# A graph-network layer: message groups in pairs, and a second layer with the features on partitions

## The chip, the cores and the metric

The kernel runs on one core of a Trainium2 chip, in one launch. The metric is the time of one execution on the device, in microseconds, as the median of several runs. A profiled execution gives the span (from the first to the last recorded instruction) and the trace from which the durations below come.

## The reference, cut to what matters

12,500 nodes with 64 features, 200,000 edges sorted by their target node. Each edge makes a message from its own features and from the features of its two nodes; messages are summed at the target node; a small network and a layer norm finish the nodes.

```python
x      (12500, 64)      edge_attr_64 (200000, 64)      edge_weight1 (200000, 1)
src, dst (200000,)      # dst is sorted
ssp(v) = softplus(v) - log(2)

nodes       = x[stack(src, dst)].reshape(E, 128)
gates       = ssp(edge_attr_64 @ We1 + be1) @ We2 + be2          # (E, 64)
gates       = gates * (1 - sigmoid(5 * (edge_weight1 - 3.5)))    # the cut
h           = ssp(nodes @ Wn1 + bn1) @ Wn2 + bn2                 # (E, 64)
message_sum = zeros(12500, 64).at[dst].add(h * gates)
new_state   = x + (ssp(message_sum @ Ws1 + bs1) @ Ws2 + bs2)
out         = layernorm(x + new_state)
```

## The kernel before

**Tiling.** Edges are worked off in 391 groups of 512 (`NG`). A group is two halves of 256 edges (`HE`); in each half the targets fall in a window of 42 consecutive nodes (`W`). Edges of a group also stand as four tiles of 128 (`K`), edge on the partition. All values are float32.

**A group's way.** Source rows come in by `gather`: four indirect DMAs on POOL (L231), one for each tile of 128 edges, into a buffer `xg` of which there are `AHEAD + BEHIND` = 19. Some 47 of the 1564 tiles are brought row by row by small DMAs on the queues of SP and ACT (`fetch`, L257). VectorE writes a one-hot of the target in its window beside the rows (`onehot`, L293). PE transposes the four tiles of 106 columns (`transposes`, L307), and ACT copies the result from PSUM to SBUF (`xcopy`, L314, the tile `xT`). Layer 1 is then feature-major, features on partitions and edges along the free side: a bias matmul of three bf16 pieces (`layer1_bias`, L319), the edge part (`layer1_edge`, L324) and two node matmuls (`layer1_node`, L330) whose weights `wns` hold Wn1's source half and, below it, 42 rows of a table `x @ Wn1` (target half) for the window; the one-hot rows pick from it. The table is made in the prologue (L591) and its rows are loaded by SP (L286).

Softplus is exp (`exps`, L341) and log with a bias of one (`logs`, L344) on ACT over 768 columns, and one min/max operation on VectorE (`softplus`, L349).

Layer 2 of before is edge-major: the softplus tile is the stationary operand and the small weights move, 2 matmuls for the edge net (L361) and 4 for the node net (L366), onto a bias matmul of 512 columns (L354). VectorE multiplies by the cut (`hcut`, L375) and makes the message (`message`, L379). PE sums the messages into the windows with the one-hots as moving operand (`scatter`, L383), and VectorE adds each half's 42 columns to the running sums (`window`, L400), whose address is read from a table of window bases.

**The order of the work.** Engines' queues are in the order in which the code is written. The loop `for i in range(-1, last - 1)` issues layer 1 of group i+1, layer 2 of group i and the scatter of group i-2, so that a group's parts are spread over three turns. In the last `CLOSE` = 12 turns the scatter is one group behind instead. `load(i + LOADS)` puts edge features and window tables on SP's queue five groups ahead, behind a scatter long past. `gather(i + AHEAD)` stands fourteen groups ahead on POOL; a buffer of rows is free again when the scatter of the group 19 before has read its one-hots. Row DMAs on ACT's queue stand between its activations (`fetch(i, 1, 3)`), on SP's seven to a group. As node sums become complete, 25 node blocks of the last network and the layer norm (`node_block`, split in parts that `BLOCK_STEPS` spreads) are put between the groups. The last groups are finished after the loop by code of their own.

PSUM: `z_tile` (layer 1, two banks), `gh_tile` (layer 2) and `tx_tile` (transposes) come from rotating pools. The scatter's result uses free columns of a `z_tile`.

Of the kernel before, what the change touches and what calls it, by code (L numbers as in the profile page):

```python
# [42 lines left out]
F32 = mybir.dt.float32  # L43
# [4 lines left out]
OP = mybir.AluOpType  # L48
# [19 lines left out]
LOADS = 5  # L68
SPREADS = 5
PREPARE = 5  # L70
BEHIND = 5
CLOSE = 12


BLOCK_STEPS = ((2, 3, 4, 4, 6, 7, 8, 9, 10, 14), (2, 3, 3, 4, 5, 6, 7, 8, 9, 10), (1, 2, 1, 2, 3))
# [48 lines left out]
def gnn_resnorm_kernel(ctx: ExitStack, tc: tile.TileContext, a: dict, out: bass.AP, E: int):  # L124
# [53 lines left out]
    one = const.tile([P, 1], F32, name="one")  # L178
    half = const.tile([P, 1], F32, name="half")
    eps = const.tile([P, 1], F32, name="eps")  # L180
    ones3 = const.tile([PIECES, HE], BF16, name="ones3")
    be3 = const.tile([PIECES, 2, D], BF16, name="be3")
    row3 = const.tile([PIECES, 2, K, D], BF16, name="row3")
    rs3 = const.tile([PIECES, K, D], BF16, name="rs3")
    wns = const.tile([DW, REST, 2, 2 * D], F32, name="wns")

    xgs, xrs, eTs = {}, {}, {}
    made = {}

    def note(key, ins):  # L190
# [80 lines left out]
    bases = {}  # L271

    def load(g):
        old = ("scatter", g - LOADS - 4)
        if g % 2 == 0:
            n = min(2, NG - g)
            both = loads.tile([P, 2, HE], F32, name="eT", bufs=4)
            behind(note(("load", g), nc.sync.dma_start(both[:, :n], a["eT"][:, g : g + n, :])), old)
            for j in range(n):
                eTs[g + j] = both[:, j]  # L280
            _, at = nc.values_load_multi_w_load_instructions(
                base_i[32:33, 2 * g : 2 * g + 4], engines=[SP], min_val=0, max_val=8 * D * (N - 1),
                skip_runtime_bounds_check_because="they were clamped to these bounds")
            bases[g], bases[g + 1] = at[:2], at[2:]
        for h in range(2):
            behind(note(("load", g), nc.sync.dma_start(  # L286
                wns[D:DW, g % REST, h, :].bitcast(U8),
                table_bytes[:, bass.ds(bases[g][h], 8 * D * W)].rearrange("o (w f) -> (o w) f", w=W))), old)
# [27 lines left out]

    def layer1_bias(g, *needs):
        zs[g] = z_tile()
        first = nc.tensor.matmul(zs[g][:, 0, :HE], be3.rearrange("q h d -> q (h d)"), ones3, start=True, stop=False,  # L319
                                 skip_group_check=True)  # L320
        behind(first, *needs)

# [14 lines left out]

    def exps(g, part=every):
        if part.start == 0:
            us[g] = work.tile([P, 3 * HE], F32, name="u")  # L340
        nc.scalar.activation(us[g][:, part], z_of(g)[:, part], AF.Exp)  # L341

    def logs(g, part=every):
# [1 line left out]

    def softplus(g, part=every):
        if part.start == 0:
            ss[g] = work.tile([P, 3, 2, P], F32, name="s", bufs=3)
        nc.vector.scalar_tensor_tensor(ss[g].rearrange("p i t e -> p (i t e)")[:, part], us[g][:, part], BIG,  # L349
                                       z_of(g)[:, part], OP.min, OP.max)  # L350

# [23 lines left out]
        nc.vector.tensor_mul(hs[g], ghs[g][:, 1], cut[:, g, :].to_broadcast([P, K, D]))  # L375

    def message(g):
        msgs[g] = work.tile([P, K, D], F32, name="msg", bufs=3)
        nc.vector.tensor_mul(msgs[g], ghs[g][:, 0], hs[g])  # L379

    def scatter(g, sc):
# [13 lines left out]
    def window(g):  # L395
        if g not in window_at:
            window_bases(g)
        for h in range(2):
            part = sums[h * D : (h + 1) * D, bass.ds(window_at[g][h], W)]
            nc.vector.tensor_add(part, part, scs[g][h * D : (h + 1) * D, h * W : (h + 1) * W])  # L400

    def node_block(first, n, pool):

# [86 lines left out]
    with tc.manual_schedule():  # L490
# [4 lines left out]
        with tc.tile_pool(name="prep", bufs=1) as prep:  # L495
# [81 lines left out]
                    nc.vector.tensor_sub(rest, rest, pieces[:, q, :])  # L577
            nc.scalar.dma_start(row_d.rearrange("(o q) f -> o q f", o=1), pieces)
            rows = prep.tile([PIECES, 4, D], BF16, name="rows")
            nc.scalar.dma_start(rows.rearrange("q i d -> q (i d)"), row_d)  # L580
            for i in range(3, PARTS):
                load_x(i)
# [3 lines left out]
            for i in range(PARTS):  # L586
                for c in range(i * CP, (i + 1) * CP, CP // 2):
                    m = CP // 2
                    ps = z_tile().rearrange("p b (k f) -> p (b k) f", k=K)
                    for k in range(m):  # L590
                        nc.tensor.matmul(ps[:, k, :], xT[:, c + k, :], wnb, start=True, stop=True)  # L591
                    tb = prep.tile([P, m, 2 * D], F32, name="tb", bufs=6)
                    nc.scalar.copy(tb[:, :K, :], ps[:, :K, :])
                    nc.vector.tensor_copy(tb[:, K:, :], ps[:, K:m, :])
                    nc.sync.dma_start(by_node[:, c : c + m], tb)
                    nc.vector.memset(sums[:, c * P : WIDE if c + m == NCH else (c + m) * P], 0.0)
                if i == 1:
                    nc.vector.tensor_copy(base_i[:1], base_b[:1])
                    nc.vector.tensor_scalar(base_i[32:33], base_b[32:33], float(8 * D), None, OP.mult)
                    nc.vector.tensor_scalar(rows_i, rows_i, float(4 * D), None, OP.mult)  # L600
                    for k in range(2):
                        nc.vector.tensor_copy(be3[:, k, :], rows[:, 0, :])
                    for k in range(K):
                        nc.vector.tensor_copy(row3[:, :, k, :], rows[:, 1:3, :])
                        nc.vector.tensor_copy(rs3[:, k, :], rows[:, 3, :])
                if i == 2:
                    nc.scalar.activation(dist, dist, AF.Sigmoid, bias=steep, scale=-5.0)
                    nc.scalar.preload_act_table_set("natural_log_exp_and_others")
                    nc.vector.tensor_copy(rel, dst_i)
                    for t in range(2):  # L610
                        r = rel[:, :, 2 * t : 2 * t + 2]
                        nc.vector.tensor_sub(r, r, base_b[:, :NH].rearrange("p (g h) -> p g h", h=2))


        with tc.tile_pool(name="finish", bufs=1) as finish:
            blocks = list(zip(node_blocks(N), block_steps(N, NG)))
            last = NG - 1
            parts, begun, complete, rest = {}, None, 0, []

            def at(f, g, *more):  # L620
                if 0 <= g < NG:
                    f(g, *more)

            def behind_by(i):
                close = last - CLOSE
                return [g for g in ([i - 2] if i <= close else []) + ([i - 1] if i >= close else []) if g >= 0]

            for g in range(LOADS - 1):
                load(g)
            for g in range(2):  # L630
                onehot(g)
            for i in range(-1, last - 1):
                now = parts.pop(i, [])
                early = [part for part in now if part.tensor]
                at(load, i + LOADS)
                read_rows(i, 0, ROWS[0])
                fetch(i, 0, ROWS[0])
                if i >= 0:
                    at(gather, i + AHEAD)
                transposes(i + 1, ("load", i + 1), ("gather", i + 1), ("onehot", i + 1))  # L640
                xcopy(i + 1)
                read_rows(i, 1, ROWS[1])
                fetch(i, 1, ROWS[1] - 6)
                layer1_bias(i + 1)
                at(layer2_bias, i)
                for n, g in enumerate(behind_by(i)):
                    scatter(g, zs[i + 1][:, 1, HE + 2 * n * W : HE + 2 * (n + 1) * W])
                layer1_edge(i + 1)
                layer1_node(i + 1)
                exps(i + 1)  # L650
                fetch(i, 1, 3)
                logs(i + 1)
                fetch(i, 1, 3)
                for g in behind_by(i):
                    window(g)
                at(layer2, i)
                for part in early:
                    part.tensor(tx_tile())
                at(hcut, i)
                at(message, i)  # L660
                softplus(i + 1)
                for part in early:
                    part.others()
                at(onehot, i + 3)
                for part in now:
                    if not part.tensor:
                        part.others()
                complete = i
                if blocks and complete >= blocks[0][1] - PREPARE and not begun:
                    begun = node_block(*blocks[0][0], finish)  # L670
                    begun.pop(0).others()
                if blocks and complete >= blocks[0][1]:
                    steps = next(steps for steps in BLOCK_STEPS if i + steps[-1] < last - 1)
                    for n, part in zip(steps, begun):
                        parts.setdefault(i + n, []).append(part)
                    rest = begun[len(steps) :]
                    blocks.pop(0)
                    begun = None
            assert len(blocks) == 1 and begun and not parts


# [43 lines left out]
    with tc.If(far > 0), tc.tile_pool(name="outside", bufs=1) as o:  # L725
# [7 lines left out]
        with tc.For_i(0, NG, 1) as g:  # L733
# [20 lines left out]
            for k in range(K):  # L754
# [1 line left out]
            xT = o.tile([P, NB], F32, name="xT2")  # L756
            nc.vector.tensor_copy(xT, z[:, 0, :])
            z = z_tile()
            nc.tensor.matmul(z[:, 1, :HE], be3.rearrange("q h d -> q (h d)"), ones3, start=True, stop=False,
                             skip_group_check=True)  # L760
            nc.tensor.matmul(z[:, 1, :HE], we1.rearrange("a h d -> a (h d)"), e, start=False, stop=True,
                             skip_group_check=True)
# [110 lines left out]
```

## Time and profile before

| What | Value |
|---|---|
| time, median of 3 runs | 2687.81 us (2668.61 to 2691.71) |
| the profiled execution's own time | 2686.47 us |
| its span | 2684.7 us |
| mean granted TensorE clock | 0.815 of full speed |
| PE busy | 2243.6 us (84%), 11373 matmuls |
| ACT busy | 969.6 us (36%) |
| DVE (VectorE) busy | 1052.4 us (39%) |
| POOL busy | 1441.8 us (54%), 1520 instructions |
| first copy of xT, last copy of xT | 143.3 us, 2660.5 us |
| last gather ends | 2586.9 us |

A profile line of a group reads: line, engine, operation, what it writes and reads, shape, count; then busy time and mean ns of one; then the idle time of the engine just before such instructions, and what ended most of it. "PEld" are the weight loads of PE, "ACTq" and "SPq" the queues' issues. "remote" is a release that the profile can't put down to an instruction. The granted clock tells how much of TensorE's full speed the chip allowed; a busy share means less at half clock.

### The profile page before, as it was taken

To read this page: it belongs to the slowest core of one execution; us is meant where nothing else is said; L and a number is where in the kernel's file an instruction comes from. 1 tells how busy PE (TensorE), PEld (TensorE's weight loads), DVE (VectorE), ACT (ScalarE), POOL (GpSimd) and SP (SyncE) were. 2 spreads that over 40 slices of the span, in tenths; PEclk is the share of its full clock that TensorE was granted. 3 is DMA by queue.
4 is the path that set the end of the run, shared out by engine and by line. 5 is a ranking of instruction groups with operands and counts; after the bars stand their busy time and mean duration, and the time that the engine had idled before them with its cause. 6 is when DMAs were issued, how large, how long until landed. Compare 5 with 4: busy or idle time off the path is not lost.

```text
span 2684.7 us, 47845 instructions
## 1 busy us (share of the span) xinstructions
PE 2243.6 (84%) x11373; PEld 1754.9 (65%) x11373; DVE 1052.4 (39%) x2767; ACT 969.6 (36%) x1318; POOL 1441.8 (54%) x1520
## 2 busy tenths in 40 slices
PE   2489888988888888888889788888888888888897
PEld 1467666766666666666667666666666667666676
DVE  1233333333334333344333443434433443444445
ACT  0133333333333333333333333333334333333344
POOL 7335555555555555555555555555555555555520
PEclk9987788788788778788777888778878887787878
DMA  6222222222222212222222222222222222222210
GB/s 159 82 64 52 48 51 49 48 49 48 49 52 50 49 47 51 51 52 47 52 46 50 51 49 53 53 50 53 51 50 50 50 58 48 54 52 50 52 44 25
DMA packets 150911, 143.53 MB, mean 53 GB/s; under 512 B 51887, under 2 KB 98395, under 8 KB 150626
## 3 DMA queue, kind: packets, MB, share of 16 engines
q1 hardware_dynamic: 94090, 88.26, 11.6%
q0 software_dynamic: 48512, 49.77, 9.5%
q10 hardware_dynamic: 8024, 2.37, 0.4%
q8 instruction: 97, 1.59, 0.2%
q14 instruction: 188, 1.54, 0.2%
HBM read 130.59 MB, written 9.63 MB: 52 GB/s over the span
## 4 chain that ended last, share of the span: by engine, by line
PE 64%; another core or an unknown queue 11%; ACTq 10%; ACT 7%; issue 5%; DVE 1%; DMA 0%; DVEq 0%; SPq 0%
PE z L330 16%; PE gh L366 12%; PE z L383 10%; ACTq L257 10%; PE gh L361 7%; PE tx L307 6%; ACT xT L314 6%; PE z L324 4%; PE gh L354 3%; PE z L319 2%; PE tx L419 1%; PE z L591 1%; ACTq L245 1%; PE tx L450 1%
## 5 line engine op out<-in xcount | busy, mean ns | idle before, releaser
L231 POOL DMA_INDIRECT xg<-in_x,src_i x1516 | 1441.6, 951 | 1144.8 <-PE z L383 353.1
L330 PE MATMUL z<-xT,wns 106*128 106x256 f32 x1564 | 574.1, 503 | 322.9 <-ACT xT L314 309.5
L330 PEld LDWEIGHTS z<-xT,wns 106*128 106x128 f32 x1564 | 361.3, 246 | 486.6 <-ACT xT L314 407.9
L341 ACT ACTIVATE u<-z 128x768 f32<-128x768 f32 x392 | 317.4, 810 | 830.4 <-issue 362.4
L366 PE MATMUL gh<-consts,s 128*128 128x64 f32 x3128 | 493.1, 313 | 0.0
L400 DVE TENSOR_TENSOR sums<-sums,z 64x42 f32 x778 | 153.0, 197 | 863.4 <-issue 626.8
L366 PEld LDWEIGHTS gh<-consts,s 128*128 128x128 f32 x3128 | 490.2, 238 | 0.1
L314 ACT COPY xT<-tx 106x512 f32<-106x512 f32 x391 | 228.9, 586 | 670.9 <-remote 231.5
L375 DVE TENSOR_TENSOR h<-gh,cut 128x256 f32<-128x256 f32 x391 | 166.1, 425 | 618.2 <-PE z L383 239.7
L344 ACT ACTIVATE u<-u,one 128x768 f32<-128x768 f32 x392 | 365.9, 934 | 69.7 <-issue 53.3
L349 DVE SCALAR_TENSOR_TENSOR s<-u,z 128x768 f32<-128x768 f32 x392 | 369.4, 943 | 11.1 <-ACT u L344 9.8
L361 PEld LDWEIGHTS gh<-consts,s 128*128 128x128 f32 x1564 | 304.0, 247 | 70.1 <-DVE s L349 32.8
L383 PEld LDWEIGHTS z<-xg,msg 128*128 128x128 f32 x1556 | 240.3, 221 | 152.8 <-issue 148.5
L361 PE MATMUL gh<-consts,s 128*128 128x128 f32 x1564 | 313.8, 335 | 1.8 <-DVE s L349 1.8
L383 PE MATMUL z<-xg,msg 128*128 128x84 f32 x1556 | 306.2, 327 | 0.9 <-DVE msg L379 0.2
L324 PE MATMUL z<-eT,consts 128*128 128x256 f32 x782 | 295.4, 465 | 0.0
L307 PE MATMUL tx<-consts,xg 128*106 128x128 f32 x1517 | 278.6, 312 | 6.4 <-DMA wns<-table 6.4
L307 PEld LDWEIGHTS tx<-consts,xg 128*106 128x106 f32 x1517 | 216.0, 169 | 10.6 <-issue 8.0
L379 DVE TENSOR_TENSOR msg<-gh,h 128x256 f32<-128x256 f32 x391 | 166.0, 425 | 13.4
L354 PE MATMUL gh<-row,ones 3*128 3x512 bf16 x391 | 170.0, 435 | 0.0
L324 PEld LDWEIGHTS z<-eT,consts 128*128 128x128 f32 x782 | 141.7, 226 | 1.2 <-issue 1.2
L293 DVE TENSOR_TENSOR xg<-consts,rel 128x168 f32<-128x168 f32 x391 | 129.9, 332 | 0.0
(93 smaller groups left out, 609.5 us busy)
## 6 DMA issues: line engine op xcount, KB each, us to landing
xr<-in_x ACTq DMA_DIRECT2D x3328, 0.2 KB
eT<-in_eT SPq DMA_DIRECT2D x195, 256.0 KB
xr<-in_x SPq DMA_DIRECT2D x2688, 0.2 KB
xg<-in_x,src_i POOLq DMA_INDIRECT x1516
wns<-table SPq DMA_DIRECT2D x782, 21.0 KB
table<-tb SPq DMA_DIRECT2D x14, 448.0 KB
sums<-in_xT SPq DMA_DIRECT2D x7, 455.0 KB
y<-in_x SPq DMA_DIRECT2D x24, 128.0 KB
```

The costliest lines, as they stand in the source:

```text
L231: note(("gather", g), nc.gpsimd.indirect_dma_start(out=xg[:, k, :D], out_offset=None, in_=x, in_offset=bass.IndirectOffsetOnAxis(ap=src_i[ ...
L257: ins = queues[queue].dma_start(row_tiles[n, "in"][r : r + 1, :D].bitcast(U8), x_bytes[:, bass.ds(row_at[queue].pop(0), 4 * D)])
L307: ins = nc.tensor.transpose(tx[:, k, :], xgs[g][:, k, :DW], ident)
L314: note(("xcopy", g), nc.scalar.copy(xT, xTs[g]))
L324: nc.tensor.matmul(zs[g][:, 0, :HE], we1.rearrange("a h d -> a (h d)"), eTs[g], start=False, stop=True, skip_group_check=True)
L330: nc.tensor.matmul(zn, wns[:, g % REST, h, :], xTs[g][:, h], start=True, stop=True, skip_group_check=True)
L341: nc.scalar.activation(us[g][:, part], z_of(g)[:, part], AF.Exp)
L344: nc.scalar.activation(us[g][:, part], us[g][:, part], AF.Ln, bias=one)
L349: nc.vector.scalar_tensor_tensor(ss[g].rearrange("p i t e -> p (i t e)")[:, part], us[g][:, part], BIG, z_of(g)[:, part], OP.min, OP.max)
L361: nc.tensor.matmul(v[:, 0, t], ss[g][:, 0, t, :], we2, start=False, stop=False, skip_group_check=True)
L366: nc.tensor.matmul(ghs[g][:, 1, 2 * t + h, :], ss[g][:, 1 + h, t, :], wn2, start=False, stop=h == 1 and t == 1, skip_group_check=True)
L383: ins = nc.tensor.matmul(sc, msgs[g][:, 2 * t : 2 * t + 2, :].rearrange("p h f -> p (h f)"), xgs[g][:, 2 * t : 2 * t + 2, D:DW], start=t = ...
```

## The change

Groups up to the 372nd go in pairs (`PAIRS` = 186), groups 2p and 2p+1 together, in a new loop over p; from there on a loop of single groups like the one before, with the scatter one group behind all along (`CLOSE` is gone). Its first turn also finishes what the last pair left.

In a pair, edge bias and edge layer 1 are one matmul each over 512 edges. The node parts stay four matmuls of 256. Exp, log and softplus run on 1024 columns (both groups' edge part and the first group's node part) and on 512 (the second group's). In ACT's order log stands directly behind exp, with three row DMAs between.

Layer 2 of a pair is feature-major: the weights are stationary, and 512 edges move. `pair_gates` is one matmul with the edge weights in block form; `pair_hidden` two matmuls of 64 output partitions each, for the two halves of the edges. The bias comes with the copy out of PSUM on ACT (`pair_bias`) and in VectorE's product (`pair_products`); the bias matmul L354 and one product are gone. Four transposes (`pair_turn`) bring the product back to edge-major, and VectorE weighs it with the cut (`pair_weigh`). The scatter is a pair behind (p-1), two groups in one turn, and four window additions follow with one read of four bases.

The row buffers are 20 instead of 19 (`BEHIND` 6), a load stands behind a scatter four groups older, and the prologue makes the two bias columns `sides2`. Number and size of gathers, row DMAs and loads stay.

The pair loop, cut to its order, with the new functions:

```diff
-BEHIND = 5
-CLOSE = 12
+BEHIND = 6
+PAIRS = 186
...
-        old = ("scatter", g - LOADS - 4)
+        old = ("scatter", g - LOADS - 8)
...
+    def pair_edge(p):
+        z1s[p] = z_tile()
+        nc.tensor.matmul(z1s[p][:, 0], be3.rearrange("q h d -> q (h d)"), ones3, start=True, stop=False,
+                         skip_group_check=True)
+        nc.tensor.matmul(z1s[p][:, 0], we1.rearrange("a h d -> a (h d)"), eT2s[p], start=False, stop=True,
+                         skip_group_check=True)
+
+    def pair_node(p, j):
+        z = (z2s if j else z1s)[p]
+        for h in range(2):
+            nc.tensor.matmul(z[:, 1, h * HE : (h + 1) * HE], wns[:, (2 * p + j) % REST, h, :], xTs[2 * p + j][:, h],
+                             start=True, stop=True, skip_group_check=True)
...
+    def pair_exps(p, j):
+        u2s[p, j] = work.tile([P, (2 if j else 4) * HE], F32, name=f"u{j}", bufs=1)
+        nc.scalar.activation(u2s[p, j], pair_z(p, j), AF.Exp)
+
+    def pair_logs(p, j):
+        nc.scalar.activation(u2s[p, j], u2s[p, j], AF.Ln, bias=one)
...
+    def pair_gates(p):
+        gates2[p] = gh_tile()
+        nc.tensor.matmul(gates2[p], we2.rearrange("a h d -> a (h d)"), s2s[p][:, :NB], start=True, stop=True,
+                         skip_group_check=True)
+
+    def pair_hidden(p):
+        hidden2[p] = gh_tile()
+        nodes = s2s[p][:, NB:].rearrange("p (j h e) -> p h j e", j=2, h=2)
+        for h in range(2):
+            nc.tensor.matmul(hidden2[p][h * D : (h + 1) * D].rearrange("p (j e) -> p j e", j=2), wn2, nodes[:, h],
+                             start=True, stop=True, skip_group_check=True)
+
+    def pair_bias(p):
+        turned2[p] = work.tile([P, NB], F32, name="mT")
+        nc.scalar.activation(turned2[p], gates2[p], AF.Identity, bias=sides2[:, 0:1])
+
+    def pair_products(p):
+        nc.vector.scalar_tensor_tensor(turned2[p], hidden2[p], sides2[:, 1:2], turned2[p], OP.add, OP.mult)
+
+    def pair_turn(p):
+        for t in range(K):
+            part = slice(t * P, (t + 1) * P)
+            nc.tensor.transpose(hidden2[p][:, part], turned2[p][:, part], ident)
...
+    def pair_scatter(p, sc):
+        for j in range(2):
+            msgs[2 * p + j] = msg2s[p][:, j]
+            scatter(2 * p + j, sc[:, j * 2 * W : (j + 1) * 2 * W])
...
+            for p in range(-1, PAIRS):
+                i, m, single = 2 * p, 2 * p + 2, p == PAIRS - 1
+                now = [parts.pop(i, []), parts.pop(i + 1, [])]
+                for j in range(2):
+                    at(load, i + LOADS + 1 + j)
+                for j in range(2):
+                    read_rows(i + j, 0, ROWS[0])
+                    fetch(i + j, 0, ROWS[0])
+                    if p >= 0:
+                        at(gather, i + AHEAD + j)
+                transposes(m, ("load", m), ("gather", m), ("onehot", m))
+                xcopy(m)
...
+                    pair_edge(p + 1)
+                if p >= 0:
+                    pair_gates(p)
+                    pair_bias(p)
+                if p >= 1:
+                    pair_weigh(p - 1)
+                fetch(i, 1, 3)
...
+                    pair_node(p + 1, 0)
+                    pair_exps(p + 1, 0)
+                fetch(i, 1, 3)
+                transposes(m + 1, ("load", m + 1), ("gather", m + 1), ("onehot", m + 1))
...
+                if p >= 0:
+                    pair_hidden(p)
...
+                    pair_products(p)
...
+                    pair_logs(p + 1, 0)
+                    xcopy(m + 1)
+                    z2s[p + 1] = z_tile()
...
+                if p >= 1:
+                    pair_scatter(p - 1, zs[m + 1][:, 1, HE:] if single else z2s[p + 1][:, 0])
+                if p >= 0:
+                    pair_turn(p)
...
+                    pair_node(p + 1, 1)
+                    pair_exps(p + 1, 1)
+                    fetch(i + 1, 1, 3)
+                    pair_logs(p + 1, 1)
+                    pair_softplus(p + 1, 0)
...
+                if p >= 1:
+                    pair_windows(p - 1)
...
+                    pair_softplus(p + 1, 1)
```

## The prediction

> **What bounds the kernel now.** I began with the page's engine shares and its chain, because they seem to give a simple answer.
>
> ```profile
> span 2684.7 us, 47845 instructions
> PE 2243.6 (84%) x11373; PEld 1754.9 (65%) x11373; DVE 1052.4 (39%) x2767; ACT 969.6 (36%) x1318; POOL 1441.8 (54%) x1520
> PEclk9987788788788778788777888778878887787878
> PE 64%; another core or an unknown queue 11%; ACTq 10%; ACT 7%; issue 5%; DVE 1%; DMA 0%; DVEq 0%; SPq 0%
> ```
>
> PE is busy 84% and makes up 64% of the chain, but its granted clock is only 0.7 to 0.8 in the loop: a stretch at half clock looks busier with the same work. So I asked for the groups and what ended the idle time before them.
>
> ```profile
> L231 POOL DMA_INDIRECT xg<-in_x,src_i x1516 | 1441.6, 951 | 1144.8 <-PE z L383 353.1
> L330 PE MATMUL z<-xT,wns 106*128 106x256 f32 x1564 | 574.1, 503 | 322.9 <-ACT xT L314 309.5
> L314 ACT COPY xT<-tx 106x512 f32<-106x512 f32 x391 | 228.9, 586 | 670.9 <-remote 231.5
> ```
>
> PE's node layer waits 309.5 us for the copy of xT, and ACT idles 670.9 us before that copy: a third of its releases are "remote", a third come from PE. The copy waits only for the transposes (L307), so I read two full-clock groups in the timeline (start, duration, instruction, idle before).
>
> ```profile
> 1380.23 0.95 POOL L231 DMA_INDIRECT xg<-in_x,src_i  x1 [1.38 <-PE z L383]
> ...
> 1382.81 0.60 PE L307 MATMUL tx<-consts,xg 128*106 128x128 f32 x4
> ...
> 1383.98 0.95 POOL L231 DMA_INDIRECT xg<-in_x,src_i  x1 [0.31 <-issue]
> ...
> 1386.15 0.59 ACT L314 COPY xT<-tx 106x512 f32<-106x512 f32 x1 [1.23 <-remote]
> ...
> 1386.46 0.94 POOL L231 DMA_INDIRECT xg<-in_x,src_i  x1 [1.54 <-remote]
> ...
> 1392.62 1.06 POOL L231 DMA_INDIRECT xg<-in_x,src_i  x1 [1.46 <-DVE mean L429]
> ```
>
> The transposes end at 1383.41, yet the copy starts at 1386.15, 2.74 us later and 1.22 us after the end of the fourth gather (1384.93). POOL's next run begins 0.31 us after the copy. Runs start 6.23 and 6.16 us apart: four gathers take 3 x 1.25 + 0.95 = 4.70, then 1.22 of landing, then 0.3. So PE's completions are seen only when POOL's run has landed, and the scatter (L383), whose completion frees the next rows, is among them. When the last gather is over (2586.89) the lateness is gone:
>
> ```profile
> 2588.73 0.42 PE L307 MATMUL tx<-consts,xg 128*106 128x128 f32 x1
> 2589.19 0.59 ACT L314 COPY xT<-tx 106x512 f32<-106x512 f32 x1 [1.53 <-PE tx L307]
> ```
>
> 2589.15 to 2589.19 is 0.04 us, and the next copies follow 4.4 us apart (2596.35, 2600.71). So the loop at full clock is a lock between PE and POOL's run, not PE's work. The windows view shows the other state:
>
> ```profile
> 1379.90:1386.10 6.20, 4.36 (x28) 3.35 (x28) 2.35 (x6) 3.26 (x5) 3.78 (x4) 1.00 0.16 31
> 1400.00:1410.00 10.00, 10.00 (x36) 7.97 (x36) 2.68 (x7) 2.33 (x3) 4.41 (x5) 0.50 0.18 46
> 1000.00:1500.00 500.00, 433.09 (x2173) 338.53 (x2171) 194.33 (x511) 184.55 (x248) 279.60 (x294) 0.79 0.21 50
> ```
>
> Columns are busy PE, PEld, DVE, ACT, POOL, then the clock. At half clock PE is busy without a gap. A mean clock of 0.80 is 40% of the time at half: of the loop's 2395 us (159 to 2554, 369 groups) 1437 at full clock hold 232 groups of 6.2 us, and 958 the other 137, 7.0 us each (state changes fall inside groups). So 63% of the groups are limited by the lock, 37% by PE.
>
> The whole: 143 us to the first xT copy, 369 groups at 6.49 us, a tail. The profiled execution took 2686.47, span 2684.7 and 1.8 around it; the median of the runs is 2687.8, 1.3 above. I write the new time as 143 + 186 P + 120, P being the time of a pair and 120 the single groups from the 372nd on (some 14 in the loop at 6.5, then those of the tail at 4 to 4.4 and the 24 us after the last xT). Today's time is reached at P = 13.0.
>
> **The change, part by part, for two groups.**
>
> PE. Gone: two layer-2 biases (L354, 2 x 0.43). Bias and edge layer 1 of a pair go as one of 512 columns each; columns and so time at one rate stay (L324 0.42 a group at full clock). Layer 2 of today is 12 matmuls a group with small moving sides: 0.61 + 1.00 = 1.6 by the timeline, 3.2 a pair. After: gates, one of 512 columns, 0.85 (as L324's two halves); hidden, two of 512 columns, 1.7; four transposes of messages, 0.44 to 0.6 (as L307). Together 3.0 to 3.1. So PE needs at full clock 0.1 to 0.2 us less for a pair, at half clock with gaps gone some 0.3 to 0.7; I take 0.7 for half-clock pairs, from 14.0 to 13.3. Hidden writes partitions 0 to 63 and 64 to 127 in two matmuls; no row shows such a pair at once, so 1.7 is the value, 0.85 the lower bound, 2.0 the upper.
> The Trainium skill ("TensorEngine Tiling (Array Packing)", Key Properties) says that such tiles of columns work independently and at once; by it hidden costs 0.85 and half-clock pairs lose up to twice 0.85 us more, 0.6 a pair on average (an estimate). No row here shows it.
>
> ACT. Today exp 0.81 + log 0.94 + copy 0.59, 4.66 a pair. After: copies 1.17, exp of 1024 and 512 columns, log the same, and the bias copy of 512. 1024 columns are not in the trace; the step from 512 to 768 (577 to 811 ns, 721 to 935) makes them 1.04 and 1.15. With the 512 forms and 0.58 for the bias: 5.24. Six issues of three row DMAs and the index reads stand between (0.85 to 1.09 for three in the timeline), and ACT needs 9 to 10 us a pair, less than P while it isn't late; "log at once behind exp" moves nothing past but these issues.
>
> DVE. Today softplus 1.89, h and msg 1.70, one-hots 0.66, windows 0.79: 5.04. After: softplus of 1024 and 512 (945 + 265 = 1.21, 0.68), products 0.68, weigh 0.69, the rest as before: 4.72. Off the path: DVE idles over half of the span.
>
> POOL. The same 1516 gathers. Now 7.75 come free at once per pair: 7.75 x 1.25 - 0.30 = 9.4 us of run, then 1.22 and 0.3 once in place of twice. P = 10.9 if all else hides under the run; 11.1 with the second scatter of a pair (0.2 behind the first). This is the gain: 2 x 6.2 at full clock against 11.1. Twenty row buffers instead of 19 make up for a scatter that now stands a pair behind; loads come against a scatter four groups older, so they wait less. The prologue gets two matmuls and three small copies, under 2 us beside 143.
>
> New wait: the pair's own chain. The second node layer (node1) needs the second xT copy, and that stands on ACT behind exp and log of the first 1024 columns. If these are released at the landing, then copy 0.59, node0 0.86, exp 1.04, log 1.15, copy 0.59, node1 0.86 put node1's end 5.1 us after the landing; where xT and node0 came early, 1.04 + 1.15 + 0.59 + 0.86 = 3.6 after it, some 3.4 into POOL's next run. Today completions up to about 2.4 us into a run are prompt (node layer: 1380.23 to exp at 1381.98); layer 2's, ending at 1382.97, already appear late (h at 1383.92, 3.7 into the run), in other groups at about 2.9, 4.4 or 5.1, or with the landing. Behind a late node1 queue exp1, log1, softplus1, then the next gates and hidden. The bounds are 0 (covered by the run) and 2.8 to 3.1 a pair on average (held to the landing, below). I take 4.4 in place of 3.4, 1.0 us, in half of the full-clock pairs, since L366 shows about as many prompt as late: 0.3 a pair over all. Half-clock pairs have their gap filled with PE's work, and I add nothing there.
>
> A rule speaks against my reading: the Trainium skill ("SBUF — State Buffer", Who interferes with whom) has only VectorE and GpSimd in each other's way and PE never waiting on anyone. The trace's 2.74 and 0.04 us say otherwise for completions. By the rule a pair would be POOL's 9.7 us or ACT's, and the time, an estimate, near 2070 to 2130.
>
> Sum: P = 0.63 x 11.1 + 0.37 x 13.3 + 0.3 = 7.0 + 4.9 + 0.3 = 12.2, and 143 + 186 x 12.2 + 120 = 2532; I say 2530.
>
> **The rivals.**
>
> 1. *The half clock goes too* (on the forecast's side). If the pair's steadier order keeps PE at full clock and node1 is prompt, P = 11.1 and the time 2328. For it: after the last gather the clock was 0.95 for 74 us. Against: node1 ends past 2.4 us into a run, and while a run of 9.4 us lasts PE has 7.6 us of work, so it idles more than now, and the half-clock stretches come in a loop in which it idles.
>
> 2. *The hold grows with the run* (slower). If every completion past 2.4 us is held to the landing, pairs alternate: one run of 11.3 us in which node1 just misses, and one where its release comes with the landing and copy, node, hidden and scatter (0.59 + 0.86 + 0.44 + 1.7 + 0.9, with waits 5.8) follow in the open: 17.1. P = 14.2, 2904. It decides from P = 13.0, that is once full-clock pairs take (13.0 - 4.9) / 0.63 = 12.8, or 1.7 us beyond the run. For it: in the prologue, in one unbroken run of 65 gathers, a copy that waits for PE alone stood for 35.8 us.
>
> ```profile
> ACT tb L593 <- remote: 77.3, 4, 35.8
> ```
>
> Against: in other runs (the first eleven gathers) completions were prompt, and L366's are seen in steps within the run. The row DMAs of SP push the same way: from 2.9 us into a run on an issue takes some 0.7 us (seven took 3.8 to 4.1, the first of them fast) instead of 0.22. SP has 8.4 us of unslowed work a pair; 8 us of slowed run would do 0.31 x 8 = 2.5 of it, and 5.9 follow: P = 13.9, 2848. But SP loads five groups ahead.
>
> 3. *The lock costs the same per group*, because the two scatters of a pair release two runs with a landing each: 2 x 6.2 = 12.4 at full clock, and with half-clock pairs at 13.3 to 14.0 P = 12.7 to 13.0, 2630 to 2680. For it: each group's scatter is two matmuls of its own, and POOL waits for each group's buffer. Against: some 0.2 to 0.5 us between the two is less than one gather.
>
> **How the numbers follow.** About 1% (27 us) is what this measurement tells from no change. The forecast has 0.42, rival 1 0.11: both are faster. Rival 2 with SP's form of it has 0.38 and lies from 2715 (part of the pairs held) over 2848 and 2904 to 3000. Rival 3 has 0.09, of which 0.06 within 1% and 0.03 faster. So faster 0.56, same 0.06, slower 0.38. The forecast's own range goes from no late node1 and hidden at 0.85 (P = 11.5, 2400) to all full-clock pairs late by 1.0 and half-clock pairs as now (12.8, 2644). The range for 8 in 10 has to reach both sides: 2310, just under rival 1, to 2900, through most of rival 2; about 0.04 lies below and 0.15 above.
>
> **What would show it.** Right: runs of seven or eight gathers, their starts 11 to 12 us apart at full clock; one landing per pair; POOL's busy time unchanged at 1442 us; idle before the xT copy cut well below 671; PE's clock still near 0.8. Rival 1: a clock of 0.95 in the loop and runs 11.1 us apart throughout. Rival 2: exp1 or the second xT copy (L314) starting 1.2 us after a run of 9 us has ended, starts alternating near 11 and 17, "remote" waits larger than 231. Rival 3: runs of four. SP's form: the transposes waiting for wns or eT. Wrong altogether: a pair limited by ACT (no idle before L449 and L424).

## The result, and the profile after

The changed kernel took 3072.07 us (median, 3064.05 to 3082.11) beside 2682.27 of the kernel before on the same chip: 1.146 times as long, 95% interval 1.1393 to 1.1526. The profiled execution's span is 3074.8 us. The first copy of xT starts at 157.4 us (143.3 before), and from the copy of group 372 to the end it is 119.8 us. From the copy of group 2 to that of group 372 are 185 pairs: 15.07 us each, where before had 13.05 for two groups.

The page first, the lines that answer to those of before.

```profile
span 3074.8 us, 40976 instructions
PE 2056.6 (67%) x7841; PEld 1215.8 (40%) x7841; DVE 1018.7 (33%) x2398; ACT 1072.5 (35%) x1504; POOL 1436.9 (47%) x1520
PEclk9987777776777777777777777787777877777778
PE 4%; issue 3%; SPq 2%; DVE 1%; POOL 1%; ACTq 0%; ACT 0%; another core or an unknown queue 0%; DMA 0%; DVEq 0%; POOLq 0%
L232 POOL DMA_INDIRECT xg<-in_x,src_i x1516 | 1436.7, 948 | 1540.6 <-DVE mT L452 534.6
L309 PE MATMUL tx<-consts,xg 128*106 128x128 f32 x1517 | 290.4, 320 | 400.0 <-DMA wns<-table 320.8
L316 ACT COPY xT<-tx 106x512 f32<-106x512 f32 x391 | 224.4, 574 | 496.6 <-PE tx L309 209.2
```

PE is busy 187 us less than before, POOL as long as before, and yet POOL idles 1540.6 us in place of 1144.8. ACT's idle time before the copy of xT fell from 670.9 to 496.6, as forecast. What is new stands on the transposes: 400.0 us of idle time, where before had 6.4. Their line of before:

```profile
L307 PE MATMUL tx<-consts,xg 128*106 128x128 f32 x1517 | 278.6, 312 | 6.4 <-DMA wns<-table 6.4
```

The chain of the page accounts for little of this span (its shares sum to about 11%) and tells nothing here. The view of waits has PE's longest waits (line waited for: us in total, times, longest):

```profile
PE tx L309 <- DMA wns<-table: 320.8, 64, 11.6
PE gh L457 <- DVE mT L452: 175.9, 62, 5.2
PE tx L306 <- DMA xr<-in_x: 175.5, 20, 12.8
```

The DMAs of the first and the third line are SP's: the window tables that it loads five to seven groups ahead, and the rows that it brings one by one (the 20 waits fall on 20 of SP's 21 row tiles). All transposes together have 569 us of idle time before them in the loop, 3.1 us a pair; 45.5 us of it are waits for a gather's landing. SP's queue is late. Its timeline, in a stretch where POOL's runs go from 1370.8 to 1380.5 and from 1383.6 to 1393.2, shows why:

```profile
1378.03 5.22 SPq L258 DMA_DIRECT2D xr<-in_x  x7
1384.19 2.99 SPq L258 DMA_DIRECT2D xr<-in_x  x7
1387.91 0.02 SPq L279 DMA_DIRECT2D eT<-in_eT  x1
1390.86 4.72 SPq L288 DMA_DIRECT2D wns<-table  x4
```

The first seven row DMAs begin late in a run and take 5.2 us; the trace has four of them start at 1378.03, 1379.47, 1381.61 and 1382.34, since SP starts an instruction only about every 0.72 us there and a row needs two, a move of its address and the DMA itself. The next seven, from 1384.19, fall into the first 3 us of the second run: at first 0.32 to 0.36 us a row. From 1386.4, 2.8 us into that run, SP is slow again, and the four loads take 4.7 us. After the run, at 1396.56, fourteen row DMAs take 5.74 us.

**Two kinds of chips.** The runs below fell on several chips. On two of them the kernel before took 1935 to 1940 us, on the others 2624 to 2692, as in the result above. The same program ran on both; each comparison is with the kernel before on its own chip, and I call them quick and late chips. Each chip of the experiments was used at one time only, so a property of the chip isn't told apart from a condition of the moment. Page of the changed kernel on a quick chip:

```profile
span 1937.2 us, 40976 instructions
PE 1670.1 (86%) x7841; PEld 1024.2 (53%) x7841; DVE 1019.8 (53%) x2398; ACT 1069.9 (55%) x1504; POOL 1442.0 (74%) x1520
PEclk9999999999999999999998999999999999999998
L232 POOL DMA_INDIRECT xg<-in_x,src_i x1516 | 1441.8, 951 | 465.4 <-issue 329.3
```

POOL's gathers there follow each other 1.25 us apart nearly without a pause, from 3.2 to 1907.7 us (its idle time is mostly the 0.30 us between two gathers, "issue"), and the clock is nearly full (0.98 on average).

### The profile page after: what moved, and what is told of

The parts are those of the page before. It is cut to its first block, busy times and chain, and to the rows that moved or that the text cites. A ratio compares the mean times of both kernels' runs of the same rounds, so it can differ in the third digit from the quotient of the medians.

```text
span 3074.8 us, 40976 instructions
## 1 busy us (share of the span) xinstructions
PE 2056.6 (67%) x7841; PEld 1215.8 (40%) x7841; DVE 1018.7 (33%) x2398; ACT 1072.5 (35%) x1504; POOL 1436.9 (47%) x1520
## 5 line engine op out<-in xcount | busy, mean ns | idle before, releaser
L232 POOL DMA_INDIRECT xg<-in_x,src_i x1516 | 1436.7, 948 | 1540.6 <-DVE mT L452 534.6
L452 DVE SCALAR_TENSOR_TENSOR mT<-gh,sides,mT 128x512 f32<-128x512 f32 x186 | 139.7, 751 | 1436.0 <-PE gh L444 1015.1
L424 ACT ACTIVATE u<-z 128x1024 f32<-128x1024 f32 x372 | 301.4, 810 | 553.0 <-PE z L416 211.5
L432 DVE SCALAR_TENSOR_TENSOR s<-u,z 128x1024 f32<-128x1024 f32 x372 | 354.9, 954 | 216.8 <-issue 132.4
L316 ACT COPY xT<-tx 106x512 f32<-106x512 f32 x391 | 224.4, 574 | 496.6 <-PE tx L309 209.2
L427 ACT ACTIVATE u<-u,one 128x1024 f32<-128x1024 f32 x372 | 347.8, 935 | 92.3 <-issue 60.4
L449 ACT ACTIVATE mT<-gh,sides 128x512 f32<-128x512 f32 x186 | 127.8, 687 | 643.5 <-PE gh L437 247.3
L410 PE MATMUL z<-eT,consts 128*128 128x512 f32 x372 | 335.1, 999 | 0.0
L437 PE MATMUL gh<-s,consts 128*128 128x512 f32 x372 | 282.5, 853 | 0.0
L457 PE MATMUL gh<-consts,mT 128*128 128x128 f32 x744 | 137.3, 314 | 191.5 <-DVE mT L452 175.9
L444 PE MATMUL gh<-s,consts 128*64 128x512 f32 x744 | 210.5, 645 | 0.0
L461 DVE TENSOR_TENSOR msg<-gh,cut 128x512 f32<-128x512 f32 x186 | 127.2, 684 | 0.0
```

What stands on the lines that cost most here:

```text
L232: note(("gather", g), nc.gpsimd.indirect_dma_start(out=xg[:, k, :D], out_offset=None, in_=x, in_offset=bass.IndirectOffsetOnAxis(ap=src_i[ ...
L316: note(("xcopy", g), nc.scalar.copy(xT, xTs[g]))
L410: nc.tensor.matmul(z1s[p][:, 0], we1.rearrange("a h d -> a (h d)"), eT2s[p], start=False, stop=True, skip_group_check=True)
L424: nc.scalar.activation(u2s[p, j], pair_z(p, j), AF.Exp)
L427: nc.scalar.activation(u2s[p, j], u2s[p, j], AF.Ln, bias=one)
L432: nc.vector.scalar_tensor_tensor(s2s[p][:, slice(4 * HE, 6 * HE) if j else slice(0, 4 * HE)], u2s[p, j], BIG, pair_z(p, j), OP.min, OP.max)
```

## The experiments

| Run | Chip | Time, us | Before beside it | A pair or two groups, us |
|---|---|---|---|---|
| changed kernel | late | 3072.1 | 2682.3 | 15.07 |
| changed, 4 rows a group on SP | late | 2624.1 | 2654.1 | 12.62 |
| changed, no rows on SP | late | 2575.4 (2568.9 on another) | 2644.3 (2656.0) | 12.35 (12.32) |
| changed, scatter split | late | 2833.4 | 2644.3 | 13.74 |
| before, no rows on SP | late | 2583.8 | 2644.3 | 12.48 |
| changed, no gathers | late | 1933.9 | 2654.1 | 9.35 |
| before, no gathers | late | 1894.8 | 2656.0 | 9.19 |
| changed kernel | quick | 1940.9 | 1936.0 | 9.36 |
| changed, 4 rows / no rows on SP | quick | 1949.8 / 1964.6 | 1938.9 | 9.43 / 9.49 |
| before, no rows on SP | quick | 1962.4 | 1938.9 | 9.51 |
| changed, no gathers | quick | 1933.4 | 1938.9 | 9.35 |

The last column is the time from the copy of xT of group 2 to that of group 372, divided by 185.

**Fewer rows on SP.** The theory at this point: SP's queue is the limit. The rival: the pair's own chain, with PE's completions held in long runs.

```diff
-ROWS = (7, 9)
+ROWS = (0, 9)      # or (4, 9); the tiles left over are gathered by POOL
```

> The changed kernel, with the 21 tiles that SP brought row by row gathered by POOL instead (ROWS (0, 9)); 21 gathers more, 26 us of POOL. Theory SP: in a run of 8 gathers SP's instructions start about 0.72 us apart from 3 us into the run until 1 us behind it, SP needs 15 us for the 45 instructions of a pair, and PE's transposes wait for its loads (558 us of idle time before them). Without the 28 instructions of the row DMAs SP is no limit, a pair falls to 12 to 12.4 us, and the time to 2500 to 2570; idle before the transposes under 50 us. Theory hold: PE's completions that are seen late in a long run make the pair long whoever brings the rows; the time stays at 2950 to 3100.

> The changed kernel with four rows a group on SP in place of seven (nine tiles more are gathered). Theory SP: 12 instructions of a pair fewer, about 2.4 us off a pair of 15.1: 12.7 us, 2600 to 2650, idle before the transposes between that of seven rows and that of none. Theory hold: no difference beyond 11 us of gathers, 3050 to 3100.

> The kernel before, with SP's 21 tiles gathered by POOL. It has no idle time before its transposes for SP's loads, so theory SP expects no gain here: 0 to 26 us more (the added gathers), 2680 to 2715. If SP's slowed queue also holds the single groups, it gets faster by 2% or more.

These three fell on a quick chip and tell nothing of SP there: 1964.55 (ratio 1.0135, 1.0118 to 1.0151), 1949.81, and 1962.39 (1.0126, 1.0109 to 1.0143). 21 gathers more at 1.25 us are 26.3 us, and the two kernels without SP's rows took 25.7 and 23.5 longer than before. This is a kernel bound by POOL.

**The changed kernel once more.**

> The changed kernel, nothing else, once more beside the kernel before. In the first experiments the kernel before took 1938.9 us in place of 2682, its gathers ran 1.25 us apart without a pause through the whole loop (1516 x 1.25 = 1895 us), and nearly every completion of PE was prompt. Theory conditions: where completions are prompt and SP isn't slowed, both kernels are limited by POOL, and the changed one takes 1930 to 1960 us, within 1% of before; where before takes about 2680, SP's slowed queue makes the changed one 3050 to 3090. Theory kernel: the changed kernel loses about 14% to before wherever it runs, 2210 beside 1939.

On another quick chip: 1940.9 beside 1936.0, ratio 1.0028 (1.0013 to 1.0043). So the 14% is no property of the kernel alone. Theory conditions held.

**No rows on SP, on late chips.**

> The changed kernel without SP's row DMAs once more (21 tiles gathered instead). Where the kernel before takes about 1936: 1960 to 1970. Where it takes about 2682: 2500 to 2570 by theory SP, 2950 to 3100 by theory hold.

> The changed kernel without SP's row DMAs, for an interval beside the kernel before and beside the next one. Where before takes about 2660: 2560 to 2580, 3 to 4% faster than before; where before takes about 1936: 1960 to 1967, 1.3% slower, the 21 added gathers.

2568.94, and on another chip 2575.43 (ratio 0.9764, 0.9706 to 0.9822). The transposes' waits are gone; the waits of PE in the second of these:

```profile
PE gh L457 <- DVE mT L452: 182.1, 75, 4.7
PE z L416 <- ACT xT L316: 119.0, 107, 2.2
PE z L416 <- ACT u L427: 77.3, 56, 1.9
```

The transposes on its page:

```profile
L309 PE MATMUL tx<-consts,xg 128*106 128x128 f32 x1538 | 286.3, 314 | 6.6 <-DMA wns<-table 6.6
```

These 6.6 us stand before the first group; in the loop there is no idle time before the transposes, and a pair takes 12.35 us. Theory SP is right and theory hold, with 2950 to 3100, wrong. The price of SP's rows in the changed kernel is 15.07 - 12.35 = 2.7 us a pair, some 500 us (on two chips whose kernels before differ by 38 us). The clock rose with it, from 0.775 to 0.829. ACT's row DMAs stay in every run, so what they cost isn't shown.

**The same with four rows.**

> The changed kernel with four rows a group on SP in place of seven, where SP's queue is slowed. Theory SP: seven rows took 15.07 us a pair, none 12.3; a limit that goes with SP's instructions gives a pair of 12.3 to 13.2 with eight rows a pair (6 rows fewer of about 0.4 us each off 15.07), 2560 to 2720, and idle before the transposes falls from 558 us to under 150. If it were the presence of row tiles and not SP's time, it would stay over 2900. Where before takes about 1936 it takes 1950 as it did.

2624.07 (ratio 0.9889, 0.9861 to 0.9918), a pair of 12.62.

```profile
L309 PE MATMUL tx<-consts,xg 128*106 128x128 f32 x1526 | 285.5, 315 | 6.5 <-DMA wns<-table 6.5
```

Again the 6.5 us stand before the first group. So with eight rows a pair SP keeps up. The six others cost 2.45 us, 0.4 each, and the eight only 0.3 together: a limit that begins between them.

**Before without SP's rows, on a late chip.**

> The kernel before without SP's row DMAs, where before takes about 2660. Theory SP (SP is no limit for runs of four gathers): 0 to 26 us more, 2660 to 2700. If SP's slowed queue costs the single groups too, 2550 to 2620.

2583.82 (ratio 0.9793, 0.9732 to 0.9855), against the expectation of theory SP and inside the range of the other. SP's rows cost the single groups too, although no transpose of before waits for SP in the loop: 60.5 us beside the kernel before on the same chip, 0.33 us for two groups (0.57 by the two kept traces, which are of different chips). POOL's idle time, by the traces, is 1022.0 in place of 1144.8 with 21 gathers more:

```profile
L231 POOL DMA_INDIRECT xg<-in_x,src_i x1537 | 1458.3, 949 | 1022.0 <-issue 361.9
```

Through what SP's DMAs lengthen the pause between two runs there was not found. SP isn't behind there: in the trace of before SP issues the edge features (eT) of two groups 38.5 us (median) ahead of the copy of their first xT. The granted clock was higher without its rows (0.856 to 0.860 in four runs, 0.818 to 0.845 in seven of before beside them); which of the two follows from the other is open. Without SP's rows the two kernels take the same within 0.4%.

**The scatter split.** Half of a pair's rows are released half a turn later.

```diff
+                if p >= 2:
+                    pair_scatter(p - 2, z2s[p][:, 0], (1,))
+                    pair_windows(p - 2, (1,))
                 fetch(i, 1, 3)
...
-                    pair_scatter(p - 1, z2s[p + 1][:, 0])
+                    pair_scatter(p - 1, z2s[p + 1][:, 0], (0,))
```

The two window additions then read their bases each for itself, in place of one read of four.

> The changed kernel with the scatter and the window additions of a pair's second group moved half a turn later (behind the next pair's gates), so that POOL gets four rows' buffers twice a pair in place of eight once. SP keeps its 14 row DMAs a pair. Theory SP by run length (an SP instruction waits about 0.72 us from 3 us into a run until 1 us behind it): the slowed time of a pair falls from 9 to about 6 us, SP needs 12.4 to 13 us a pair as it did in the kernel before: 2570 to 2690 where before takes about 2680. Theory SP by number of DMAs alone: 3050 to 3090, as the changed kernel. Theory hold: shorter runs show PE's completions earlier, 12.4 us a pair, about 2570, with or without SP's rows. Where before takes about 1936 there are no runs to split and it takes 1935 to 1960.

2833.35 (ratio 1.0757, 1.0677 to 1.0836), between the theories' numbers, and no clean test: the waits show why.

```profile
POOL xg L232 <- DVE sums L402: 592.3, 129, 11.6
ACT u L424 <- remote: 570.5, 89, 8.4
PEld z L385 <- DVE s L432: 480.1, 94, 7.9
```

The moved scatter writes into the tile z2s of the pair whose layer 2 is under way, and so waits for that pair's second softplus (L432), which stands late on VectorE. That is a wait which the edit brought. What it does show: with 14 rows a pair still on SP, idle time before the transposes fell from 569 to 14 us. Of 266 runs in the loop (a pause of over 0.6 us ends a run) 162 have three or four gathers. But the pair took 13.74 us besides, and gave SP more time; that shorter runs alone free SP is not shown by it.

**No gathers.**

> The changed kernel with every gather replaced by a memset of the same rows on POOL, so that the source rows are zero; row DMAs, loads and all else stay. If POOL's runs of gathers slow SP's queue and delay PE's completions, both go: no SP interval of 0.7 us, no 1.2 us between the end of a run and the copy, a pair of 8.5 to 10 us, 1850 to 2150 us in all. If the pair's own chain or SP's number of DMAs is the limit by itself, the time stays over 2600.

> The kernel before with every gather replaced by a memset of the same rows on POOL (source rows are zero). The changed kernel without gathers took 9.35 us a pair, no less than with them (9.36), so its own order, with ACT's activations and row DMAs in it, is as slow as POOL. If the change makes the order of the other engines shorter, the kernel before takes more than 9.35 us for two groups here, 1940 us or more. If the change only moves work, and PE's 4.0 to 4.4 us a group of the tail behind the last gather is what before could do, two groups take 8.0 to 8.8 us and the whole 1690 to 1840. Where the gathers are what delays PE's completions, the same time comes out whether the kernel before takes 1936 or 2682 beside it.

> The changed kernel with memsets in place of the gathers, source rows zero. Where before took 2656, before without gathers took 1894.75, so the gathers cost it some 760 us there. Theory SP (SP and PE are slowed only while gathers run): 1925 to 1940, as where before took 1939, with SP's seven rows a group in place; SP's number of DMAs then costs nothing by itself. If SP's queue is slow there for another reason: over 2500.

The changed kernel took 1933.41 on a quick chip, inside the range of the first case, and 1933.92 on a late one. The kernel before took 1894.75 on a late chip, between its two expectations. Each of the three is one run. The page of the second:

```profile
span 1932.1 us, 39727 instructions
PEclk9999999999999999999999999999999999989998
L307 PE MATMUL tx<-consts,xg 128*106 128x128 f32 x1517 | 235.5, 274 | 6.5 <-DMA wns<-table 6.5
```

Without gathers the changed kernel takes the same on both kinds of chips, the clock is nearly full, and with SP's 14 rows a pair in place the idle time before the transposes is 32 us (for SP's rows) in place of 569. So on the late chips it is the gathers that slow SP and hold PE. Together with the lower clock, which isn't told apart from it, that is 1138 us of the changed kernel (3072.1 - 1933.9, two late chips) and 761 of the one before (2656.0 - 1894.8). The source rows are zero here; that this by itself raised the clock isn't excluded, but the quick chips have the same clock with the true rows.

What the other engines need for a pair these runs don't show. SP has no pause in them: between the copies of group 2 and group 372 its pauses of over 0.08 us add up to 0.09 us a pair, and it issues the edge features only 12 us ahead of the copy in the changed kernel and 5 us in the one before (medians from the 25th to the 165th pair). So 9.35 and 9.19 lie near SP's own time for its 44 and 42 instructions, some 9.2 us, and the 39 us by which the changed kernel is longer can't be put down to the change's other engines. PE's busy time alone fell, from 1771 to 1673 us.

## Why the prediction was wrong

**The sum for a pair fits the changed kernel without SP's rows, not the changed kernel.** Forecast: P = 12.2 and 2530. Without SP's rows it is 12.35, of which 0.14 are the added gathers, and 2575. Its full-clock part fits as well: 56 of 179 turns there ran at a granted clock of over 0.95 and took 11.73 us on average, beside 11.1 and 1.0 in half of the pairs, 11.6. No turn ran at half clock throughout, so 13.3 can't be read from it, and that the 1.0 is the late node layer wasn't tried. In the changed kernel runs of 7 or 8 gathers came, 8 in 138 and 7 in 38 of 179 runs between 200 and 2900 us; POOL's busy time stayed at 1437, the idle time before xT's copy fell, the clock stayed near 0.8 (0.775).

**The step that failed is in rival 2: "were SP the bound, P = 13.9, 2848. But SP loads five groups ahead."** The place was named, with the transposes' wait for wns as its mark, but two things were wrong.

The first is the "but". A lead of five groups covers a delay, not a rate. SP needs more time a pair than the pair has, falls behind, and after some pairs no lead is left. The trace shows it: SP issues the edge features (eT) of a pair up to 24 us ahead of the copy of its first xT at the start of the loop, and 6.8 us ahead (median) from the 25th pair to the 165th; with four rows a group on SP that median is 40 us, without SP's rows 44. Then the transposes wait, POOL's run with them, and SP wins some time back: 89 of 183 runs have no idle time before their transposes and are followed by the next 12.4 us after their start, the 94 others 17.7 us after it. The sum to make was SP's time per pair against P, and by the prediction's own numbers it was 13.9 against 12.2: SP was the bound by that sum, and the forecast should have been 2848 or more.

The second is the size, 13.9 where 15.07 was measured. The prediction took an issue in the slowed stretch at 0.7 us, from seven rows in 3.8 to 4.1 us. Those seven straddle the slowed stretch and the free time beside it. A row is two instructions of 0.72, 1.44 us: from 1378.03, four row DMAs start within 4.3 us. With 0.32 / 1.44 = 0.22 in place of 0.31, 8 us of slowed run do 1.8 of SP's 8.4, and 6.6 follow: 14.6. The 8.4 of unslowed work was too small as well: the runs without gathers show some 9.2, and with it the same estimate gives 15.4.

**Rival 2 as first told (held completions, pairs alternating 11 and 17) was not it.** Without SP's rows runs start 11.8 to 13.5 us apart for eight in ten, though PE's completions are still seen late there: the product (L452) starts 0.64 us behind the end of the hidden matmuls (median), and in a tenth of the pairs 3.9 us or more.

**Rival 3** (two runs a pair) is excluded by the runs of 7 and 8. **Rival 1** had the clock go up; it didn't.

**Prologue.** Two matmuls and three copies were put at under 2 us; the first xT copy came 14 us later. The new bias columns' matmul (L682) stood 57.4 us for its operand (rows, L679), in a prologue that one unbroken run of gathers covers. That this moved the start was not tried by itself.

**PE.** Hidden was taken at 1.7, bounds 0.85 to 2.0. In the timeline of the changed kernel its four records (two matmuls, two records each) take what two of gates (one matmul) take:

```profile
1414.13 1.02 PE L437 MATMUL gh<-s,consts 128*128 128x512 f32 x2
...
1416.81 1.08 PE L444 MATMUL gh<-s,consts 128*64 128x512 f32 x4
```

The rule of the Trainium skill ("TensorEngine Tiling (Array Packing)", Key Properties), that tiles of columns work at once, holds here: 1.08 us, where one after the other would be 2 x 1.02, against the value that was chosen. PE's saving was mis-added besides: 3.2 + 0.86 against 3.0 to 3.1 is 1.0 us a pair less, not 0.1 to 0.2, since the two biases were left out. Neither is what made the kernel slower.

**The other rule** of the skill ("SBUF — State Buffer", Who interferes with whom), that PE never waits on anyone, is said there of the engines' ports to SBUF; the prediction held it against the late completions. On the quick chips gathers go on all the time and PE's completions are prompt: the changed kernel's product starts 0.13 us behind the hidden matmuls in nine pairs of ten. On a late chip, in before, the copy of xT starts 0.73 us behind the transposes where ACT was free (median of 171), and 0.04 us without gathers (median of 100). What holds PE's completions on the late chips while gathers run stays open; that it is a port to SBUF isn't shown. The estimate by that rule, 2070 to 2130, was too high for the quick chips because their prologue is 61 us shorter (first xT copy at 82.2) and a pair took 9.36 in place of 9.7.

**Smaller readings.** Of the 670.9 us before the copy of xT, PE's releases end two thirds (217.1, 212.4 and 6.4), not a third. The parts named for the 120 us of single groups add up to over 130, though 119.8 was measured. Behind the last gather the first two copies of xT are 7.2 us apart, and the mean over all of them is 4.8, not 4.4.

What makes a chip quick or late stays open. The profile before was of a late chip, and the lock that the prediction read in it belongs to that kind.

## What to carry to other kernels

A queue that runs ahead is judged by its time per turn against the turn, not by its lead; do that sum for every queue whose issues are slowed by what the change makes longer. A group of issues whose mean mixes a slowed and a free stretch is split before its rate is used. And when one stretch of waiting looks like a property of the chip, run the kernel before on another chip as well: here the change made the time 0.3% longer on one kind and 14.6% on the other, and the better kernel on the late chips (the changed one without SP's rows, 0.976) was the worse one on the quick (1.0135).

## What the hardware showed beyond expectation

On late chips, SP's instructions start about 0.72 us apart from about 3 us into a run of gathers until about 1.2 us behind its last gather. In the loop of the changed kernel 1018 of 8108 such intervals lie between 0.68 and 0.76 us, 950 of them from 2.6 us into a run to 1.4 us behind it; on the quick chip 8 of 8114, and without gathers on a late chip 9 of 8112. ACT's queue, whose three row DMAs the prediction took at 0.85 to 1.09 us, is slowed there as well: in the changed kernel's run from 1410.9 to 1420.7 three row DMAs took 0.9 us at 1412.73 and at 1413.72, but 3.19 at 1415.64 and 2.84 at 1419.58. The gathers themselves take the same 0.95 us on both kinds (951 ns on the page of either). Without gathers, the kernel before takes 1894.75 us on a chip where it takes 2656.02 with them.
